# A two-layer graph attention kernel: the first attention's projection by seven half-size products (Strassen, Winograd's form) instead of eight

## The chip, the core and the metric

The kernel runs on one core of a Trainium2 chip. A core has TensorE (PE, matrix products out of SBUF into PSUM), VectorE (DVE), ScalarE (ACT), GpSimd (POOL) and SyncE (SP, here only a queue that issues DMAs). Each engine takes its instructions in the order of the program and waits for semaphores of the others. The metric is the device time of one execution in microseconds; smaller is better. Everything is in fp32.

## The reference, cut to what matters

Sixteen batches, each 1024 nodes with 256 features, go through a layer of two attentions with a residual (`_L0_gnn_ref`) and a layer of one (`_L1_gnn_ref`). The change touches only the first projection in the first layer, `h = inp @ W`, and what hangs on it:

```python
out = relu(x @ mlp1_w + mlp1_b)          # (16, 1024, 512): the kernel's resT, transposed
h = out @ W_fc                           # 1024x512 by 512x512: the projection
f1, f2 = h @ a[:512], h @ a[512:]
e = leaky_relu(f1[:, :, None] + f2[:, None, :], 0.2)    # no mask here
att = softmax(e, axis=2)
h_prime = elu(att @ h)
out = elu(h_prime) + out                 # merged into resT
out = relu(out @ mlp2_w + mlp2_b)        # then the masked attention "a", then layer 1 with "b"
```

## The kernel before

**Tiles.** A batch has NT = 8 tiles of P = 128 nodes. `wfc_sb` is W_fc in four chunks of 128 rows (HC = 4) and two halves g = 0, 1 of 256 columns; each half has one column more (F + 1 = 257), which holds W_fc times a half of `a`, so that f1 comes out as the last column of g = 0 and f2 as that of g = 1. A half of one tile of h is a PSUM group of four matmuls 128x128 by 128x257 (`Dense.project`, L470), and ACT copies it to `h_nat` (L472). For g = 0 POOL takes f1 to `fs` (L474) and puts ones in its place (L475). An fp32 matmul is two rows in the profile.

**The dense attention has no mask**, and is not computed as a matrix: nodes are sorted by f2. `columns` (L478) takes f2 and its maximum, `send` (L243 to L246) turns f2 into a row through PE, ACT and a DMA to DRAM, `row` (L489) brings it back in all partitions, `highest` (L501) finds the maximum over partitions, and `rank` (L514 to L523, once a tile, on DVE) counts how many are smaller. `scatter` (L530, on POOL) writes the rows of h in sorted order to DRAM, `read_sorted` reads them, `sum_before` and `sum_behind` make weighted sums from both ends on DVE, `write_table` and `carry` put these into tables in DRAM, and `gather` (L642, on POOL) fetches for each node the row at its place; `share` (L654) and `mean` (L664 on ACT, L667 on DVE) make the quotient, and `merge` / `merge_end` (L714 to L725) transpose it, apply elu twice and add it to `resT`. `sign` (L553, on ACT) finds each node's place, and needs its f1 from `fs` and the row of f2. `mlp2` (L732) follows. Then come `m.project` of the masked attention "a" (L322, copies on ACT L324), its weights (L375) and products (L385), and the second layer "b" in the same manner. `Norm` makes the layer norm: `stats` (L262), `root` (POOL), `center` (`hn`, L272, DVE) and `turn` (transposes, L282, called nt).

**Order.** All batches are pipelined. Each step is put into one list with a number, `at(lo, hi, steps)`, the list is sorted by that number, and this is the order of the instructions on PE, DVE, ACT, SP and also on POOL. The numbers only order; they are not times. A batch has PERIOD = 142 of them, `base_of(b)` is where the masked part of batch b begins, and a dense part is spread over two periods: for batch b + 2, `dense_rows` puts the projections g = 1 at 86 to 99.5 after `base_of(b)`, and `dense_begin`, with t0 = `base_of(b + 1)`, puts `columns` at t0 - 38.5, `send` and `row` at t0 - 36.8, two projections g = 0 at t0 - 33, `highest` at t0 - 31.5, ranks from t0 - 28 to t0 - 12 and the other six g = 0 at t0 - 21 to t0 - 8. In the same places stand, for batch b + 1, `share` and `mean` at 78 and 92, `merges` at 85 and 98.2, `mlp2` at 102.5 to 116.5 and `m.project` at 135 to 142, and, for batch b + 3, the norm: stats at t0 - 33.5 and t0 - 13, `turn` of the first half at t0 - 22 and of the second at t0 + 0.2, with its `center` 4 before. Batches 0 and 1 are done in a prologue with an order of its own (START).

**Buffers.** PSUM: `mm` four buffers of one bank, used in turn by all products; `tr` two; `bc` one of two banks, used by `send`, `carry` and broadcasts. SBUF: `att` eight tiles of 128x256 for weights of the attentions; `work` has two `part` tiles and two `carry` tiles.

## Time and profile before

| what | value |
|---|---|
| median of 3 runs | 2345.46 us (2337.66 to 2345.5) |
| span of the profiled execution | 2331.2 us, granted clock 0.997 |
| instructions | 30884 |
| projection, matmuls (L470), 2048 rows | 465.7 us busy |
| projection, copies on ACT (L472), 256 | 93.1 us busy, mean 366 ns |
| projection, f1 on POOL (L474 and L475), 128 each | 24.5 and 12.6 us |
| masked products (L385), "b" and "a" | 462.8 and 454.6 us |
| POOL's adds 128x256 (L413), 118 | 98.7 us, mean 836 ns |
| DVE's adds 128x256 (L431), 128 | 54.6 us, mean 427 ns |
| reads and writes of HBM | 226.88 and 126.29 MB |

The span is from the first to the last instruction; the median is 14.3 us above it and the lowest run 6.5 us. A row of a group of instructions names line, engine, operation, out<-in, shapes and count, then busy time and the mean of one in ns, then the time for which the engine stood idle just before them and what ended it. Matmuls overlap, so the busy time of a group of them divided by its count is the time from one to the next, and is smaller than the mean of one. In a timeline the columns are start and length in us, engine, line, operation and count, and in brackets the idle time before and its releaser.

### The profile page before, as it was taken

The page shows a single profiled execution, that of the slowest core. Times are in us where ns is not written, and L with a number is a line of the kernel's source. Part 1 is how long each engine was busy: PE and PEld are TensorE (multiplying, and loading weights), DVE is VectorE, ACT ScalarE, POOL GpSimd, SP SyncE. Part 2 cuts the span into 40 slices and gives each one's busy share as a digit, 9 for nine tenths or more (in the row PEclk, how much of TensorE's full clock was granted, in tenths as well). Part 3 has the DMA queues.
Part 4 walks back from the last instruction along what each step waited for, and adds up shares of the span by engine and source line. Part 5 has one row for each costly group of instructions (what it writes and reads, how often), then busy time and mean ns, then how long its engine had stood idle before and what let it go on. Part 6 is the DMA issues. An engine that isn't in the chain of part 4 may idle for free. (4 is left out here: it accounts for less than half of the span.)

```text
span 2331.2 us, 30884 instructions
## 1 busy us (share of the span) xinstructions
PE 2260.4 (97%) x9962; PEld 1742.7 (75%) x9962; DVE 1625.0 (70%) x4535; ACT 1240.5 (53%) x2745; POOL 950.8 (41%) x1212
## 2 busy tenths in 40 slices
PE   8999999999999999999999999999999999999898
PEld 5666787777868778787776868778786777878666
DVE  6676785766858667675766858567785866858655
ACT  5355645547365563745546365563745547364442
POOL 1153435264443536335263433636335263533420
PEclk9999999999999999999999999999999999999999
DMA  4658356572656736366572756647366582646500
GB/s 172 171 164 208 75 175 168 167 187 88 200 139 178 184 135 183 105 187 153 176 197 89 195 123 181 181 146 182 97 192 160 164 201 101 195 101 191 138 21 27
DMA packets 150714, 355.28 MB, mean 152 GB/s; under 512 B 11200, under 2 KB 62728, under 8 KB 146448
## 3 DMA queue, kind: packets, MB, share of 16 engines
q1 hardware_dynamic: 103936, 189.06, 28.2%
q0 software_dynamic: 45952, 163.99, 26.6%
q8 instruction: 82, 1.34, 0.2%
q14 instruction: 88, 0.72, 0.1%
q10 hardware_dynamic: 656, 0.17, 0.0%
HBM read 226.88 MB, written 126.29 MB: 151 GB/s over the span
## 5 line engine op out<-in xcount | busy, mean ns | idle before, releaser
L385 PE MATMUL ob<-hmb,attb 128*128 128x257 f32 x2048 | 462.8, 383 | 10.8 <-DVE attb L375 6.7
L470 PE MATMUL h<-wfc_sb,resT 128*128 128x257 f32 x2048 | 465.7, 380 | 0.0
L385 PE MATMUL oa<-hma,atta 128*128 128x258 f32 x2048 | 454.6, 381 | 3.4 <-DVE atta L375 3.3
L385 PEld LDWEIGHTS ob<-hmb,attb 128*128 128x128 f32 x2048 | 383.1, 190 | 77.3 <-ACT rb L427 9.6
L385 PEld LDWEIGHTS oa<-hma,atta 128*128 128x128 f32 x2048 | 387.8, 190 | 62.9 <-DVE atta L375 4.5
L470 PEld LDWEIGHTS h<-wfc_sb,resT 128*128 128x128 f32 x2048 | 379.4, 190 | 53.5 <-issue 0.7
L725 POOL TENSOR_TENSOR resT<-resT,e 128x512 f32<-128x512 f32 x128 | 163.7, 1279 | 367.0 <-DVE e L724 325.7
L375 DVE SCALAR_TENSOR_TENSOR atta<-rowsa,qwda,edge 128x256 f32<-128x256 f32 (+1 forms) x520 | 269.0, 547 | 25.0 <-PE oa L385 12.3
L413 POOL TENSOR_TENSOR posa<-posa,onat 128x256 f32<-128x256 f32 x118 | 98.7, 836 | 459.5 <-ACT posa L401 459.4
L375 DVE SCALAR_TENSOR_TENSOR attb<-rowsb,qwdb,edge 128x256 f32<-128x256 f32 (+1 forms) x536 | 248.2, 505 | 8.9 <-PE ob L385 5.5
L456 PE MATMUL m<-hT,w_sb 128*128 128x512 f32 x512 | 236.0, 600 | 0.6 <-ACT posa L401 0.6
L427 ACT ACTIVATE rb<-ob,recb 128x256 f32<-128x256 f32 x128 | 59.0, 475 | 332.7 <-DVE recb L425 323.1
L732 PE MATMUL m<-resT,w_sb 128*128 128x512 f32 x512 | 228.3, 593 | 2.2 <-POOL resT L725 2.2
L642 POOL DMA_INDIRECT got<-coarse,k x124 | 201.3, 1623 | 38.6 <-issue 37.9
L400 ACT ACTIVATE ea<-oa,reca 128x256 f32<-128x256 f32 x128 | 60.7, 474 | 270.7 <-DVE reca L397 262.0
L716 DVE TENSOR_SCALAR e<-hpT 128x512 f32<-128x512 f32 x128 | 88.3, 690 | 129.9 <-PE hpT L714 97.0
L732 PEld LDWEIGHTS m<-resT,w_sb 128*128 128x128 f32 x512 | 93.8, 191 | 103.7 <-issue 91.3
L642 POOL DMA_INDIRECT got<-fine,k x124 | 125.3, 1010 | 104.5 <-DVE attd L688 43.8
L456 PEld LDWEIGHTS m<-hT,w_sb 128*128 128x128 f32 x512 | 92.7, 193 | 96.6 <-issue 92.7
L530 POOL DMA_INDIRECT sorted<-hnat,place x128 | 131.9, 1031 | 39.6 <-issue 21.1
L553 ACT ACTIVATE junk<-r,fs 128x1024 int8<-128x1024 f32 x124 | 142.5, 1149 | 6.8 <-POOL fs L474 5.3
L717 ACT ACTIVATE e<-e 128x512 f32<-128x512 f32 x128 | 80.7, 630 | 82.1 <-DVE e L716 82.0
(189 smaller groups left out, 3443.2 us busy)
## 6 DMA issues: line engine op xcount, KB each, us to landing
xs<-sorted SPq DMA_DIRECT2D x32, 1028.0 KB
fine<-tt SPq DMA_DIRECT2D x32, 1026.0 KB
fine<-xs SPq DMA_DIRECT2D x32, 1026.0 KB
x<-in_x_dram SPq DMA_DIRECT2D x16, 1024.0 KB
xn<-in_x_dram SPq DMA_DIRECT2D x15, 1024.0 KB
out_dram<-x SPq DMA_DIRECT2D x28, 512.0 KB
coarse<-carry SPq DMA_DIRECT2D x32, 256.5 KB
r<-row_r SPq DMA_DIRECT2D x14, 512.0 KB
```

What stands on the lines that cost most here:

```text
L375: nc.vector.scalar_tensor_tensor(a_t[:, :n * P], self.rows[:, i], self.qwd[:, 1, j:j + 1], edge[:, j, i], op0=OP.max, op1=OP.mult)
L385: nc.tensor.matmul(self.out[t][:, :F + self.ONES], lhsT=self.att[t0, j][:, (t - t0) * P:(t - t0 + 1) * P], rhs=self.hm[:, j, 2:2 + F + sel ...
L413: adder.tensor_add(pos, pos, o_nat[:, t, :])
L456: nc.tensor.matmul(ps, lhsT=w1_sb[:, kc, c * P:(c + 1) * P], rhs=hT[:, kc, h * HALF:(h + 1) * HALF], start=(kc == 0), stop=(kc == FC - 1))
L470: nc.tensor.matmul(ps[:, :F + 1], lhsT=self.resT[:, kc, t * P:(t + 1) * P], rhs=wfc_sb[:, kc, g, :], start=(kc == 0), stop=(kc == HC - 1))
L530: made = nc.gpsimd.indirect_dma_start(out=sorted_d[self.b % 2], out_offset=bass.IndirectOffsetOnAxis(ap=self.place[:, t:t + 1], axis=0), i ...
L553: nc.scalar.activation(junk, self.r2, AF.Sign, bias=self.fs[:, 0, t:t + 1], accum_out=self.signs[:, t:t + 1])
L642: nc.gpsimd.indirect_dma_start(out=got[u // n][:, u % n, :], out_offset=None, in_=(coarse_d if coarse else fine_d)[self.b % 2][:, :], in_o ...
L716: nc.vector.tensor_scalar_min(e, ps, 0.0)
L717: nc.scalar.activation(e, e, AF.Exp)
L725: nc.gpsimd.tensor_add(dst, dst, e)
L732: nc.tensor.matmul(ps, lhsT=w2_sb[:, kc, c * P:(c + 1) * P], rhs=self.resT[:, kc, h * HALF:(h + 1) * HALF], start=(kc == 0), stop=(kc == H ...
```

## The change

With A = resT transposed, cut in halves of nodes (1, 2) and of channels, and B = W_fc with its two extra columns, cut in the same way, the four quarters of h = A B are made from seven products instead of eight:

- sums of A, for each of four row blocks u (`sums_of`): S1 = A21 + A22 and S2 = S1 - A11 on DVE, S3 = A11 - A21 and S4 = A12 - S2 on POOL, 128x256 each, into `att` tiles, which become 257 wide;
- sums of B, once (`seven_weights`, four subtractions on POOL); six of the seven factors stay in SBUF, the seventh, B21, goes to DRAM and is loaded again for each batch (`load_b21`, two DMAs of 131.6 KB on SP);
- products (`step`): each is two matmuls 128x128 by 128x257. Steps 1, 6, 5, 3 of a block add into one PSUM buffer, and ACT copies what stands there after each of them to a quarter of `h_nat`. Step 7 of two blocks goes into a `bc` buffer, and `add_pair` adds it on DVE to two quarters (two instructions 128x514 a pair). Steps 2 and 4 have a buffer of their own and are added on DVE to g = 0; f1 and the ones follow on POOL.

Steps 1, 7, 6, 5, 3 (20 a batch) stand at 85.3 to 108 where g = 1 stood; steps 2 and 4 (8 a batch) stand where g = 0 stood, at t0 - 31 and t0 - 22 to t0 - 10. `columns`, `send`, `highest` and the ranks move 4 to 5.7 places back, scatters 2.5, `read_sorted` 2.5, the sums 1.5 to 2, the second `mlp2` 0.7, the `send` of "b" from lo + 24 to 97.3 after `base_of(b)`. The `carry` tiles, the lines and `zero` take `part` tiles.

```diff
+    wfc_more = const.tile([P, 2, 2, F + 1], F32, name="wfc_more")
+    wfc_d = dram.tile([P, 2 * (F + 1)], F32, name="wfc_d")
+
+    def seven_weights():
+        top, low = slice(0, 2), slice(2, HC)
+        b11, b12, b21, b22 = [wfc_sb[:, k, g, :] for k in (top, low) for g in range(2)]
+        nc.sync.dma_start(wfc_d.rearrange("p (k f) -> p k f", k=2), b21)
+        nc.gpsimd.tensor_sub(wfc_more[:, 1], b22, b12)
+        nc.gpsimd.tensor_sub(b12, b12, b11)
+        nc.gpsimd.tensor_sub(wfc_more[:, 0], b22, b12)
+        nc.gpsimd.tensor_sub(b21, b21, wfc_more[:, 0])
...
+    def att_tile(name):
+        return big.tile([P, F + 1], F32, tag="att", name=name, bufs=ATT)
...
-        line = work.tile([NT, P], F32, tag="carry", name=name, bufs=2)
+        line = work.tile([NT, P], F32, tag="part", name=name)
...
-            a_t = big.tile([P, PAIR], F32, tag="att", name=f"att{self.name}_{t0}_{j}", bufs=ATT)
+            a_t = att_tile(f"att{self.name}_{t0}_{j}")
...
-        def project(self, t, g):
+        def sums_of(self, u, which):
+
+            if self.s is None:
+                self.s, self.chain, self.b21 = {}, {}, None
+            one, two = slice(u * P, (u + 1) * P), slice(HALF + u * P, HALF + (u + 1) * P)
+            a11, a12 = self.resT[:, 0:2, one], self.resT[:, 2:HC, one]
+            a21, a22 = self.resT[:, 0:2, two], self.resT[:, 2:HC, two]
+            t = self.s[which, u] = att_tile(f"s{which}_{self.b}_{u}")[:, :PAIR].rearrange(
+                "p (k n) -> p k n", k=2)
+            if which == 1:
+                nc.vector.tensor_add(t, a21, a22)
+            elif which == 2:
+                nc.vector.tensor_sub(t, self.s[1, u], a11)
+            elif which == 3:
+                nc.gpsimd.tensor_sub(t, a11, a21)
+            else:
+                nc.gpsimd.tensor_sub(t, a12, self.s[2, u])
+
+        def load_b21(self):
+            self.b21 = [att_tile(f"b21_{self.b}_{k}") for k in range(2)]
+            for k in range(2):
+                nc.sync.dma_start(self.b21[k], wfc_d[:, k * (F + 1):(k + 1) * (F + 1)])
+
+        def multiply(self, ps, lhs, rhs, start):
+            for k in range(2):
+                nc.tensor.matmul(ps, lhsT=lhs[:, k, :], rhs=rhs[k], start=start and k == 0,
+                                 stop=k == 1, skip_group_check=True)
+
+        def step(self, i, u):
 
             if self.h_nat is None:
                 self.h_nat = big.tile([P, NT, 2, F + 1], F32, tag="seq", name=f"hnat_{self.b}",
                                       bufs=2)
                 self.fs = small.tile([P, 2, NT], F32, tag="fs", name=f"fs_{self.b}")
-            ps = mm_psum(f"h_{self.b}_{t}_{g}")
-            for kc in range(HC):
-                nc.tensor.matmul(ps[:, :F + 1], lhsT=self.resT[:, kc, t * P:(t + 1) * P],
-                                 rhs=wfc_sb[:, kc, g, :], start=(kc == 0), stop=(kc == HC - 1))
-            nc.scalar.copy(self.h_nat[:, t, g, :], ps[:, :F + 1])
-            if g == 0:
-                nc.gpsimd.tensor_copy(self.fs[:, 0, t:t + 1], self.h_nat[:, t, 0, F:])
-                nc.gpsimd.memset(self.h_nat[:, t, 0, F:], 1.0)
+            top, low = (0, 1), (2, 3)
+            b = {1: [wfc_sb[:, k, 0, :] for k in top], 2: self.b21,
+                 3: [wfc_sb[:, k, 1, :] for k in low], 4: [wfc_sb[:, k, 0, :] for k in low],
+                 5: [wfc_sb[:, k, 1, :] for k in top], 6: [wfc_more[:, 0, k, :] for k in top],
+                 7: [wfc_more[:, 1, k, :] for k in top]}[i]
+            one, two = slice(u * P, (u + 1) * P), slice(HALF + u * P, HALF + (u + 1) * P)
+            a = {1: lambda: self.resT[:, 0:2, one], 2: lambda: self.resT[:, 2:HC, one],
+                 3: lambda: self.s[4, u], 4: lambda: self.resT[:, 2:HC, two],
+                 5: lambda: self.s[1, u], 6: lambda: self.s[2, u], 7: lambda: self.s[3, u]}[i]()
+            h = self.h_nat
+            if i in (1, 6, 5, 3):
+                if i == 1:
+                    self.chain[u] = mm_psum(f"h_{self.b}_{u}")
+                ps = self.chain[u][:, :F + 1]
+                self.multiply(ps, a, b, i == 1)
+                t, g = {1: (u, 0), 6: (u + TH, 0), 5: (u + TH, 1), 3: (u, 1)}[i]
+                nc.scalar.copy(h[:, t, g, :], ps)
+            elif i == 7:
+                if u % 2 == 0:
+                    self.pair = bc_psum(f"h7_{self.b}_{u}")
+                self.multiply(self.pair[:, u % 2 * HALF:u % 2 * HALF + F + 1], a, b, True)
+            else:
+                ps = mm_psum(f"h{i}_{self.b}_{u}")[:, :F + 1]
+                self.multiply(ps, a, b, True)
+                t = u if i == 2 else u + TH
+                nc.vector.tensor_add(h[:, t, 0, :], h[:, t, 0, :], ps)
+                nc.gpsimd.tensor_copy(self.fs[:, 0, t:t + 1], h[:, t, 0, F:])
+                nc.gpsimd.memset(h[:, t, 0, F:], 1.0)
+
+        def add_pair(self, u):
+            ps = self.pair.rearrange("p (u f) -> p u f", u=2)[:, :, :F + 1]
+            for g in (1, 0):
+                dst = self.h_nat[:, TH + u:TH + u + 2, g, :]
+                nc.vector.tensor_add(dst, dst, ps)
...
-            carry = work.tile([P, K], F32, tag="carry", name=f"carry_{self.b}_{s}", bufs=2)
+            carry = work.tile([P, K], F32, tag="part", name=f"carry_{self.b}_{s}")
...
     def dense_rows(t0, b):
 
-        for t in range(NT):
-            at(t0 + BETWEEN[t], t0 + BETWEEN[t], [partial(dense[b].project, t, 1)])
+        d = dense[b]
+        for lo, u, i in ((84, 0, 3), (84.5, 1, 3), (86.2, 0, 1), (86.3, 0, 2), (87.4, 1, 1),
+                         (87.5, 1, 2), (88.5, 0, 4), (89.5, 1, 4), (91, 2, 3), (92, 3, 3),
+                         (95.8, 2, 1), (95.9, 2, 2), (97, 3, 1), (97.1, 3, 2), (99, 2, 4),
+                         (100, 3, 4)):
+            at(t0 + lo, t0 + lo, [partial(d.sums_of, u, i)])
+        for lo, i, u in ((85.3, 1, 0), (86.2, 1, 1), (87.1, 7, 0), (88, 7, 1), (89.2, 6, 0),
+                         (90.2, 6, 1), (91.2, 1, 2), (92.2, 1, 3), (93.4, 5, 0), (94.4, 5, 1),
+                         (95.6, 3, 0), (96.6, 3, 1), (98, 7, 2), (99, 7, 3), (100, 6, 2),
+                         (101, 6, 3), (103.6, 5, 2), (104.6, 5, 3), (107, 3, 2), (108, 3, 3)):
+            at(t0 + lo, t0 + lo, [partial(d.step, i, u)])
+        for lo, u in ((96, 0), (106, 2)):
+            at(t0 + lo, t0 + lo, [partial(d.add_pair, u)])
+        at(t0 + 107.5, t0 + 107.5, [d.load_b21])
+
+    def early_steps(d, lo, hi):
+        def group(u):
+            return ([partial(d.sums_of, v, i) for v in (u, u + 1) for i in (3, 1, 2)]
+                    + [partial(d.sums_of, v, 4) for v in (u, u + 1)]
+                    + [partial(d.step, i, v) for i in (1, 7, 6, 5) for v in (u, u + 1)]
+                    + [partial(d.add_pair, u)] + [partial(d.step, 3, v) for v in (u, u + 1)])
+        at(lo, hi, group(0) + group(2))
+
+    def late_steps(d):
+        return [partial(d.step, i, u) for i in (2, 4) for u in range(TH)]
 
     def dense_begin(t0, b):
         d = dense[b]
-        at(t0 - 38.5, t0 - 38.5, [d.columns])
-        at(t0 - 36.8, t0 - 36.8, [d.send, partial(d.row, True)])
-        at(t0 - 31.5, t0 - 31.5, [d.highest])
-        at(t0 - 28, t0 - 12, each(d.rank, range(NT)))
-        at(t0 - 33, t0 - 30.5, [partial(d.project, t, 0) for t in range(2)])
-        at(t0 - 21, t0 - 8, [partial(d.project, t, 0) for t in range(2, NT)])
-        scatters(d, t0 - 18.5, t0 - 4.5)
-        at(t0 - 6, t0 - 6, [d.query])
-        at(t0 - 4, t0 - 4, [d.read_sorted])
+        at(t0 - 32.8, t0 - 32.8, [d.columns])
+        at(t0 - 31.5, t0 - 31.5, [d.send, partial(d.row, True)])
+        at(t0 - 27, t0 - 27, [d.highest])
+        at(t0 - 24, t0 - 8, each(d.rank, range(NT)))
+        late = late_steps(d)
+        at(t0 - 31, t0 - 28, late[:2])
+        at(t0 - 22, t0 - 10, late[2:])
+        scatters(d, t0 - 16, t0 - 2)
+        at(t0 - 4, t0 - 4, [d.query])
+        at(t0 - 1.5, t0 - 1.5, [d.read_sorted])
...
-        at(t0 - 3, t0 - 3, [d.sums_begin])
-        for t, lo in enumerate((27, 25, 18.5, 16.3, 14.1, 12, 9.8, 8.2)):
+        at(t0 - 1, t0 - 1, [d.sums_begin])
+        for t, lo in enumerate((24.5, 22.7, 18, 16, 14, 12, 9.8, 8)):
             at(t0 - lo, t0 - lo, [partial(d.sign, t)])
         for h in range(2):
-            at(t0 + 6.5 + 4 * h, t0 + 6.5 + 4 * h, [partial(d.sums_weights, h)])
-            at(t0 + 7.5 + 5 * h, t0 + 12.5 + 5 * h, each(d.sum_before, tiles(h)))
-        at(t0 + 13, t0 + 13, [partial(d.write_table, 0, 0)])
-        at(t0 + 18, t0 + 18, [partial(d.write_table, 0, 1)])
-        at(t0 + 18, t0 + 32, each(d.sum_behind, range(NT - 1, -1, -1)))
-        at(t0 + 25, t0 + 25, [partial(d.write_table, 1, 1)])
-        at(t0 + 32, t0 + 32, [partial(d.write_table, 1, 0)])
-        at(t0 + 33, t0 + 33, [d.count])
+            at(t0 + 8 + 4 * h, t0 + 8 + 4 * h, [partial(d.sums_weights, h)])
...
-        for i, lo in enumerate((102.5, 104.8, 113, 116.5)):
+        for i, lo in enumerate((102.5, 105.5, 113, 116.5)):
...
-            at(lo + 24, lo + 24, [m.send])
+            at(base_of(b + 1) - 44.7, base_of(b + 1) - 44.7, [m.send])
...
-    at(START + 14.1, START + 14.1, [wfc_columns])
+    at(START + 14.1, START + 14.1, [wfc_columns, seven_weights])
...
-    at(START + 33, START + 50, each(d.project, range(NT), [1]))
+    early_steps(d, START + 33, START + 50)
+    at(START + 49, START + 49, [d.load_b21])
...
-    at(START + 50.5, START + 64, each(d.project, range(NT), [0]))
+    at(START + 50.5, START + 64, late_steps(d))
...
-    at(START + 80, START + 94, each(dense[1].project, range(NT), [1]))
-    at(START + 76, START + 82, each(d.weight, [0], range(NT)))
+    early_steps(dense[1], START + 80, START + 94)
+    at(START + 93.5, START + 96.5, each(d.weight, [0], range(NT)))
...
-        lo = START + 95 + 7.1 * t
+        lo = START + 96.5 + 6.9 * t
...
-    at(START + 123.4, START + 141, each(e.project, range(NT), [0]))
+    at(START + 118.5, START + 118.5, [e.load_b21])
+    at(START + 123.4, START + 141, late_steps(e))
```

## The prediction

> **What bounds the kernel now.** I read the page's busy times first, then the busy time of each engine in stretches of 146 us.
>
> ```profile
> PE 2260.4 (97%) x9962; PEld 1742.7 (75%) x9962; DVE 1625.0 (70%) x4535; ACT 1240.5 (53%) x2745; POOL 950.8 (41%) x1212
> 1026.00:1172.00 146.00, 144.68 (x640) 112.61 (x639) 105.28 (x291) 80.02 (x180) 63.56 (x81) 1.00 0.59 161
> ```
>
> In the second line the columns are busy PE, weight load, DVE, ACT, POOL. In a middle stretch PE is idle for 1.3 us of 146. One batch follows the next after 139.0 us (the row transposition of L243 at 963.32 and again at 1102.35). Next, the groups of instructions:
>
> ```profile
> L470 PE MATMUL h<-wfc_sb,resT 128*128 128x257 f32 x2048 | 465.7, 380 | 0.0
> L322 PE MATMUL pa<-wh_sb,oT 128*128 128x258 f32 x512 | 117.2, 383 | 1.2 <-ACT hma L324 0.9
> ```
>
> A product of L470 is two rows, and a row takes 465.7/2048 = 227 ns of PE. L322 is the nearest row for groups of two chunks, as the new steps are: 117.2/512 = 229 ns. So the rows themselves do get fewer at the same price. Where the saved time goes is read from the timeline, in the stretch from the transposition that sends f2 (call it S, L243) to the transposes of the next input's second half (call it N, L282):
>
> ```profile
> 963.32 0.27 PE L243 MATMUL line_ps<-ident,fs 128*8 128x128 f32 x1
> 965.62 0.24 ACT L245 COPY line<-line_ps 8x128 f32<-8x128 f32 x1
> 967.15 0.34 SPq L489 DMA_DIRECT2D r<-row_r  x1
> 971.15 1.28 DVE L518 TENSOR_SCALAR_CACHE_REDUCE junk<-r,fs 128x1024 uint8<-128x1024 f32 x1
> 987.21 0.22 DVE L523 SCALAR_TENSOR_TENSOR place<-rank 128x1 int32<-128x1 f32 x1
> 988.39 0.63 ACT L324 COPY hma<-pa 128x258 f32<-128x258 f32 x2
> 991.05 1.48 DVE L272 TENSOR_SCALAR hn<-xn,mv,rstd 128x256 f32<-128x256 f32 x4 [1.37 <-POOL rstd L268]
> 992.38 1.04 PE L282 MATMUL nt<-ident,hn 128*128 128x128 f32 x8
> ```
>
> From S to N PE has 29.06 us of work without a gap. Beside it runs a chain on the others: f2 goes out and comes back as a row, eight ranks run on DVE from 971.15 to 987.34, then the statistics, then hn, the last of which ends at 992.53. Both arrive at N together. That this chain has no reserve is seen one stretch later, where the row came later (S to first rank 9.36 us instead of 7.83):
>
> ```profile
> 1250.88 1.28 DVE L518 TENSOR_SCALAR_CACHE_REDUCE junk<-r,fs 128x1024 uint8<-128x1024 f32 x1 [1.53 <-DMA r<-row_r]
> 1269.92 2.01 PE L322 MATMUL pa<-wh_sb,oT 128*128 128x258 f32 x8 [0.41 <-ACT hma L324]
> ```
>
> PE waited at once. So PE is the bound, but in this stretch the rank chain is a second one, level with it.
>
> **Term 1, the products.** Per batch 64 products become 56. Before S there were 32 (g = 1): 64 x 0.2274 = 14.55 us; now steps 1, 7, 6, 5 and 3 run there, 40 products, 80 x 0.229 = 18.32: +3.77. After S there were 32 (g = 0), 14.55; now steps 2 and 4, 16 products, 32 x 0.229 = 7.33: -7.22. Net -3.46 us a batch. The saving is thus taken entirely from the stretch whose second bound is DVE, and more than it.
>
> [...]
>
> **Term 2, the wait at N.** PE now needs 29.06 - 7.22 = 21.84 us from S to N. The chain on DVE, from S:
> - To the first rank. ACT is free for the line's copy (before it stood 2 us behind exponentials), so 0.3 + 0.24 + 0.3 to the DMA's issue, 1.27 to the row's issue (965.88 to 967.15), 3.9 to landing (1246.98 to 1250.88): 6.0. The maximum (L501) stands ahead of the ranks and behind 0.27 + 1.83 (two steps) + 3.55 (mlp2) + 0.27 on PE, then about 0.7 on DVE: 6.6. I take 6.6.
> - Eight ranks: 971.15 to 987.34 less one hn (0.32): 15.85.
> - New on DVE between the ranks: six adds of step 2 and 4, 128x257 out of PSUM. Not in the trace; the nearest row is L431 (128x256, median 0.425, 0.33 from start to start): 6 x 0.38 = 2.3, bounds 2.0 and 2.6.
> - Statistics of four tiles 987.34 to 989.48: 2.14; query 0.2; the first hn 0.4.
>
> Together 27.5 us: if DVE alone decides, PE waits 27.5 - 21.8 = 5.7 us. There is a second way to count: from the first rank to N it took 21.2 us above and 20.9 where PE had waited for ACT; 6.6 + 20.9 + 2.3 = 29.8, a wait of 8.0. The reason is the queue on ACT: the copies of pa stand behind the last sign, the last sign waits for fs of the last tile, fs is copied by POOL after step 4's add, and that add stands on DVE behind seven ranks; with four mm buffers PE can't pass. Step 2's and 4's buffers are themselves released by these adds. I take 29.0, nearer to this, so 7.2 us; bounds 5.7 and 8.0. No gain is possible here: latency and ranks alone, 6.0 + 15.85, equal PE's 21.8.
>
> **Term 3, the wait at S.** Before, columns ran at 960.93, 2.4 us ahead of S. Now the last step 3 is the last work of PE before S and columns needs its copy: 0.22 + 0.36 on ACT, 0.16 on DVE, the hand-overs: 0.85 us, bounds 0.6 and 1.2. Queued behind it are steps 2 and mlp2.
>
> **Term 4, waits inside the first steps.** Steps 1, 6, 5, 3 of a row block add into one PSUM buffer, and between them ACT copies it. ACT is in order and at this place stands behind the shares of the gathers:
>
> ```profile
> 946.39 0.21 DVE L654 TENSOR_TENSOR den<-got,qd 128x4 f32<-128x4 f32 x1 [1.16 <-DMA got<-coarse,k]
> 947.85 0.63 ACT L717 ACTIVATE e<-e 128x512 f32<-128x512 f32 x1 [1.54 <-DVE e L716]
> 949.14 1.32 ACT L664 ACTIVATE part<-got,den 128x513 f32<-128x513 f32 x2
> 950.37 0.35 ACT L472 COPY hnat<-h 128x257 f32<-128x257 f32 x1
> 951.97 0.35 ACT L472 COPY hnat<-h 128x257 f32<-128x257 f32 x1
> ```
>
> The product copied at 951.97 was finished at about 949.5: 2.4 us late, at no cost, since four buffers covered it. Now step 3 of block 0 follows step 5 of block 0 with one step (0.92 us) between: wait 2.4 - 0.9 = 1.5, up to 2.7 if the copy must come after all four parts (till 952.06). Then the pair of step 7 holds the only bc buffer until DVE has done hp, merge_end, two sums and the pair's add (4 x 0.42 + 2 x 0.72 more than before); the send of row b and the third step 7 stand behind: 0 to 2.0, I take 0.5. Together 2.0, bounds 0 and 4.7.
>
> **What costs nothing.** DVE gains 8 sums, 4 pair adds and 8 adds, 8 x 0.425 + 4 x 0.72 + 8 x 0.4 = 9.5 us a batch; before S it was busy for 14.2 of 25 us (938 to 963), now some 20.5 of 29, so only order counts there. Without that cover it would cost up to 6 us. POOL gains 8 x 0.84 = 6.7 (L413), 7.6 of 25 becoming 14.3 of 29. ACT keeps 16 copies. [...] The b21 loads (263 KB) go out on SP once the fourth step 7 is done; SP sat 42 us waiting for the row (591 us over 14), and DMA moves 1 to 3 GB/s there. If they were late, step 2 would be by up to the 3.9 us of the 512 KB row. Reading the sorted rows and the sums move by 1.5 to 2.5 places, but the last scatter comes earlier against N, and DVE idled 4.45 us there for its rows; if it were late, that is the reserve. carry and line now share part's two buffers with the running total; a line is long gone when a carry needs its place, and carry (1032.65) leads the first coarse gather (1056.35) by 23 us. In the prologue PE idles 20.5 of the first 168 us, so two batches' 7 us may not pay, and POOL has four subtractions more (4 x 1.28): 0, bounds -7 and +10.
>
> **Sum.** A steady period: -3.46 + 7.2 + 0.85 + 2.0 = +6.6 us. 14 batches run so (2 to 15): +92. On the span of 2331.2: 2423; the median of the runs is 14.3 above that span (the lowest 6.5), so 2437. Bounds: -3.46 + 5.7 + 0.6 = +2.8 a period, 40 in all, 7 less in the prologue: 2378; -3.46 + 8.0 + 1.2 + 4.7 = +10.4, 146 and 10 more: 2501.
>
> **Rivals.**
> - *PE is the bound throughout, faster.* It pays 14 x 3.46 + 7 = 55 us: 2290. For it: 97%, and 1.3 us idle a period. Against it: S to N has to stay under 21.84 + 3.46 = 25.3 us; my count is 27.5 at least, and a row 1.5 us late was enough for a wait. It decides if the chain is 2.2 us shorter than counted and terms 3 and 4 are near nothing. With part of the gain: 0.14.
> - *A wash.* The chain takes about 25.5 and terms 3 and 4 little: 2345. 0.05.
> - *The PSUM chain is the main cost.* Not one but most of the twelve hand-overs a batch (6, 5, 3 in four blocks) wait for ACT, by 0.4 us more each: 5 us a period, 70 on top: 2507. Against it: the other copies lag by 0.3 to 1.5 us, with 2.7 us of other steps between. 0.07.
> - *The products get no cheaper* (two-chunk groups cost 260 ns a row): 112 x 0.26 against 64 x 2 x 0.2274 gives nothing saved, 48 us more: 2485. L322 speaks against it. 0.04.
> - *The forecast*, 2437: 0.70.
>
> Faster by over 0.5% (about what a measurement of this kernel can tell from no change): 0.14; within: 0.05; slower: 0.81. Between 2350 and 2505 lie 8 in 10.
>
> **What would show it.** Right: PE idle before L282 or L322, on DVE's hn or ACT's hma, 5 to 8 us a period; ranks starting some 6.6 us after S; PE idle before step 3 on ACT's copy. Wrong: S to N below 25 us, or no PE gap before L282 and a period under 139 us.

## The result, and the profile after

The changed kernel takes 2562.99 us (median of 4 runs, 2562.22 to 2567.52) against 2345.48 us before: ratio 1.0927, 95% interval [1.0898, 1.0955]. It is slower, by 217 us where 92 were forecast, and above the range (2378 to 2501 us). The profiled execution has a span of 2561.2 us (before 2331.2, so 230 longer) and a mean granted clock of 0.952 (before 0.997). The difference of the spans is 12.5 us larger than that of the medians, since the profiled execution before was quicker than its median by that much; spread over a period of 139 us this is some 0.7 us, so the losses of a period below are that much too high.

The page's busy times after:

```profile
PE 2319.2 (91%) x9706; PEld 1741.0 (68%) x9706; DVE 1799.3 (70%) x4855; ACT 1252.0 (49%) x2745; POOL 1058.8 (41%) x1344
```

PE has 256 instructions fewer and is busy for 59 us more, while its share fell from 97% to 91%. So two things are to be found: waits, and rows that became slower.

S (now L258, `line_ps`) comes at 305.8, 459.2, ... 2302.4 us: a period of 153.59 us against 139.24 before (the mean of 13 periods). The 230 us of span are then 39.3 up to the first S (266.5 became 305.8), 13 x 14.35 = 186.5 in the periods, and 4.3 behind the last S. From S to N (now L297) it takes 29.3 us (median; before 29.1), so next to nothing was lost there, and nothing gained; from N to the next S 124.3 in place of 110.1.

Inside N to S the loss has one place: from the first transposition of the merges (hpT) to S, where the new steps are. Busy time of this stretch and of S to N; the columns are length, busy PE, weight load, DVE, ACT, POOL, each with its count, then the granted clock. Before:

```profile
937.30:963.30 26.00, 25.66 (x116) 18.54 (x115) 14.80 (x33) 18.59 (x37) 7.64 (x6) 1.00 0.42 101
...
963.30:992.40 29.10, 29.10 (x125) 22.06 (x124) 24.55 (x85) 21.87 (x48) 13.68 (x29) 1.00 0.23 82
```

After:

```profile
1033.30:1073.30 40.00, 33.37 (x131) 23.62 (x130) 26.48 (x55) 22.56 (x46) 16.30 (x18) 0.87 0.27 67
...
1073.30:1102.40 29.10, 25.29 (x89) 17.05 (x90) 23.52 (x83) 17.91 (x37) 11.39 (x29) 0.88 0.24 83
```

26.0 us became 40.0: the whole 14 us of the period. Idle time of PE went from 0.3 to 6.6 us. Its busy time went from 25.7 to 33.4, and 16 rows more, at 227 ns each, explain only 3.6 of these 7.7: the clock is 0.87, so rows run slower in a part of the stretch. PE's timeline in this stretch, after:

```profile
1043.19 1.90 PE L502 MATMUL h<-wfc_sb,s 128*128 128x257 f32 x8
1049.78 3.77 PE L502 MATMUL h<-wfc_sb,s 128*128 128x257 f32 x8 [4.70 <-ACT hnat L527]
1053.85 0.37 PE L258 MATMUL lineb_ps<-ident,qwdb 128*8 128x128 f32 x1 [0.30 <-DVE hnat L544]
1054.65 2.05 PE L502 MATMUL h<-wfc_more,s 128*128 128x257 f32 x4 [0.44 <-ACT lineb L260]
...
1057.35 2.75 PE L502 MATMUL h<-wfc_more,s 128*128 128x257 f32 x8
...
1073.29 0.27 PE L258 MATMUL line_ps<-ident,fs 128*8 128x128 f32 x1 [0.67 <-DVE fs L547]
```

Eight rows take 1.90 us at 1043.19 (238 ns each, the first with its fill) and 3.77 at 1049.78, behind the wait of 4.70 us. The granted clock over the same time says why (the columns are those of the stretches above):

```profile
1045.00:1049.00 4.00, 0.09 (x1) 0.00 (x0) 2.40 (x4) 3.81 (x7) 1.26 (x1) 0.98 0.00 0
1049.00:1053.00 4.00, 3.22 (x8) 2.51 (x8) 3.77 (x6) 1.29 (x4) 1.73 (x2) 0.50 0.00 0
1053.00:1058.00 5.00, 4.27 (x13) 2.89 (x12) 1.80 (x5) 0.63 (x2) 1.10 (x2) 0.50 0.05 8
1058.00:1062.00 4.00, 4.00 (x17) 3.09 (x17) 1.65 (x3) 2.36 (x4) 0.00 (x0) 0.87 0.19 61
```

From about 1049 to 1059 PE runs at half speed. That costs some 4 us: 8 rows 1.9, the next 4 rows 1.0, a block of transpositions 0.5, the 8 rows at 1057.35 0.9. So the ledger of this stretch, from these views: 3.6 us of products that now stand before S, 6.3 of waits, some 4 of half clock, nothing gained behind S. It says where PE's time went, not what each entry would give back if it were gone: in the periods that end with S at 1534.1, 1840.6 and 1994.1 the clock came back sooner (0.95, 0.91 and 0.91 over the stretch, which took 37.5 to 38.0 us), and they are no shorter than the others (152.8 to 153.5 us).

The wait itself comes about as the prediction had it (step 3 waits for ACT's copy of step 5, which stands behind the second half's parts), but it is 4.7 us. DVE's shares, ahead of the parts:

```profile
1041.77 0.63 DVE L723 TENSOR_TENSOR den<-got,qd 128x4 f32<-128x4 f32 x1
1042.43 1.20 DVE L724 TENSOR_TENSOR den<-den,got 128x4 f32<-128x4 f32 x1
...
1043.88 0.44 DVE L726 TENSOR_TENSOR den<-den,qd 128x4 f32<-128x4 f32 x1
```

Three instructions on 128x4 elements take 0.44 to 1.20 us where the same took 0.17 to 0.21 before (from 946.39 on). GpSimd over the same time:

```profile
1040.96 1.42 POOL L493 TENSOR_TENSOR s<-resT,s 128x256 f32<-128x256 f32 x2
1042.33 1.28 POOL L793 TENSOR_TENSOR resT<-resT,e 128x512 f32<-128x512 f32 x1
1043.56 1.43 POOL L491 TENSOR_TENSOR s<-resT 128x256 f32<-128x256 f32 x2
```

The first share ends at 1042.40, where a subtraction of GpSimd ends (1042.38), the second at 1043.63, where the merge's addition to resT ends (1043.61; the kernel before has this one too), the last at 1044.32, about where the first of the two next subtractions ends. ACT behind them:

```profile
1046.24 0.71 ACT L733 ACTIVATE part<-got,den 128x513 f32<-128x513 f32 x1
...
1047.11 1.39 ACT L733 ACTIVATE part<-got,den 128x513 f32<-128x513 f32 x2
1048.66 0.72 ACT L733 ACTIVATE part<-got,den 128x513 f32<-128x513 f32 x1 [0.16 <-DVE hp L736]
1049.29 0.63 ACT L527 COPY hnat<-h 128x257 f32<-128x257 f32 x2
```

Step 5 was done at about 1045.1; its copies run at 1049.29, behind all four parts.

### The profile page after: what moved, and what is told of

Its sections match the earlier page's. It is cut to its first block, busy times and chain, and to the rows that moved or that the text cites. A ratio compares the mean times of both kernels' runs of the same rounds, so it can differ in the third digit from the quotient of the medians.

```text
span 2561.2 us, 31111 instructions
## 1 busy us (share of the span) xinstructions
PE 2319.2 (91%) x9706; PEld 1741.0 (68%) x9706; DVE 1799.3 (70%) x4855; ACT 1252.0 (49%) x2745; POOL 1058.8 (41%) x1344
## 5 line engine op out<-in xcount | busy, mean ns | idle before, releaser
L390 DVE SCALAR_TENSOR_TENSOR atta<-rowsa,qwda,edge 128x256 f32<-128x256 f32 (+1 forms) x520 | 261.1, 534 | 29.2 <-DMA rowsa<-row_a 14.2
L337 PE MATMUL pa<-wh_sb,oT 128*128 128x258 f32 x512 | 165.1, 478 | 54.9 <-DVE hnat L536 53.4
L502 PE MATMUL h<-wfc_sb,s 128*128 128x257 f32 x512 | 147.6, 439 | 64.8 <-ACT hnat L527 64.8
L337 PEld LDWEIGHTS pa<-wh_sb,oT 128*128 128x128 f32 x512 | 114.3, 237 | 106.0 <-DVE hnat L536 79.1
L502 PEld LDWEIGHTS h<-wfc_sb,s 128*128 128x128 f32 x512 | 109.8, 220 | 94.5 <-issue 72.9
```

What stands on the lines that cost most here:

```text
L337: nc.tensor.matmul(ps[:, :2 + F], lhsT=hT[:, c, t * P:(t + 1) * P], rhs=self.w_sb[:, c, 0, :], start=(c == 0), stop=(c == FC - 1))
L390: nc.vector.scalar_tensor_tensor(a_t[:, :n * P], self.rows[:, i], self.qwd[:, 1, j:j + 1], edge[:, j, i], op0=OP.max, op1=OP.mult)
L502: nc.tensor.matmul(ps, lhsT=lhs[:, k, :], rhs=rhs[k], start=start and k == 0, stop=k == 1, skip_group_check=True)
```

## The experiments

All runs beside the two kernels. N to S is the period less the median of S to N; the first S shows the prologue. The runs were taken on several chips, each with the kernel before beside it (2335.1 us for the a runs, 2343.4 for b, 2344.2 for c, 2344.8 for d), so the ratios compare better than the times: by them a1 is as slow as the changed kernel.

| kernel | time, us | ratio to before | period | S to N | N to S | first S |
|---|---|---|---|---|---|---|
| before | 2345.5 | 1 | 139.24 | 29.1 | 110.1 | 266.5 |
| changed | 2563.0 | 1.0927 [1.0898, 1.0955] | 153.59 | 29.3 | 124.3 | 305.8 |
| d1, before, less work behind S | 2344.5 | 0.9996 [0.9977, 1.0016] | 140.03 | 29.5 | 110.5 | 267.0 |
| d2, before, long wait | 2453.3 | 1.0446 [1.0416, 1.0476] | 148.29 | 29.1 | 119.2 | 266.7 |
| d3, before, shorter wait | 2418.3 | 1.0297 [1.0267, 1.0327] | 145.55 | 29.0 | 116.5 | 266.2 |
| a1, wait filled | 2554.5 | 1.0936 [1.0862, 1.1009] | 153.39 | 29.4 | 124.0 | 306.1 |
| a3, no adds of steps 2, 4 | 2516.0 | 1.0771 [1.0739, 1.0802] | 150.51 | 27.9 | 122.6 | 300.8 |
| b1, no sums | 2519.4 | 1.0753 [1.0709, 1.0798] | 151.11 | 30.2 | 120.9 | 295.5 |
| b2, no pair adds | 2534.4 | 1.0817 [1.0757, 1.0877] | 152.21 | 29.6 | 122.6 | 294.1 |
| b3, products only | 2485.1 | 1.0607 [1.0559, 1.0655] | 149.27 | 29.0 | 120.3 | 285.3 |
| b4, shares later | 2525.4 | 1.0779 [1.0735, 1.0823] | 150.98 | 29.5 | 121.5 | 305.9 |
| c1, row sent earlier too | 2539.8 | 1.0831 [1.0801, 1.0861] | 152.30 | 30.5 | 121.8 | 306.9 |
| a2, mlp2 behind S | 2520.2 | 1.0789 [1.0746, 1.0832] | 150.35 | 30.4 | 120.0 | 305.1 |
| c2, c1 and mlp2 behind S | 2500.6 | 1.0664 [1.0637, 1.0691] | 149.11 | 30.6 | 118.5 | 306.6 |
| c3, c2 and the old prologue | 2480.4 | 1.0574 [1.0554, 1.0593] | 149.18 | 32.3 | 116.9 | 281.2 |
| a4, the old prologue alone | 2535.2 | 1.0853 [1.0821, 1.0886] | 152.77 | 29.3 | 123.5 | 288.0 |

### What is the work behind S worth? (d1, a3)

d1 is the kernel before with half of the late products gone, about what the change takes from there (7.3 us):

```diff
-            for kc in range(HC):
+            n = 2 if g == 0 and self.b > 1 else HC
+            for kc in range(n):
```

> The kernel before, with half of the products of its late projection (the ones behind S, batches 2 to 15) left out: two of four per tile, 7.3 us of TensorE in each period behind S, output not the reference's. Nothing else is touched. Theory (behind S the chain of ranks, signs and copies ends at 28 to 29 us whatever TensorE does, so the 7.2 us of products that the change took from there are worth nothing): period 138 to 139.2, S to N 28 to 29.4, 2325 to 2345 us. Rival (TensorE set that stretch before, and only the change's adds made VectorE its bound): S to N 22 to 24 us, period 132 to 134, 2250 to 2280 us.

2344.54 us, ratio 0.9996 [0.9977, 1.0016]: nothing. PE's timeline of one S to N in d1:

```profile
966.60 0.27 PE L243 MATMUL line_ps<-ident,fs 128*8 128x128 f32 x1
...
977.13 5.37 PE L471 MATMUL h<-wfc_sb,resT 128*128 128x257 f32 x24
...
990.66 5.44 PE L322 MATMUL pa<-wh_sb,oT 128*128 128x258 f32 x16 [2.30 <-ACT hma L324]
995.94 1.03 PE L282 MATMUL nt<-ident,hn 128*128 128x128 f32 x8
```

N still comes 29.3 us after S. Of the 7.3 us left out some 4 came back as waits (of pa for ACT's signs and copies above all) and some 2 as slower rows: 16 rows of pa take 5.44 us here, where 229 ns a row makes 3.7. Meanwhile the chain on DVE runs to its end:

```profile
994.31 1.48 DVE L272 TENSOR_SCALAR hn<-xn,mv,rstd 128x256 f32<-128x256 f32 x4 [1.37 <-POOL rstd L268]
```

The last hn ends at 995.79, 29.2 us after S, and N follows at 995.94. The chain of ranks is thus a bound of its own, without any of the change's adds.

a3 leaves out the eight adds of steps 2 and 4 in the changed kernel (L536):

```diff
-                nc.vector.tensor_add(h[:, t, 0, :], h[:, t, 0, :], ps)
```

> The eight adds of steps 2 and 4 out of PSUM on DVE are left out, so the first half of h lacks these products; nothing else changes. Theory (PE waits before N because the four mm buffers are freed by adds that stand between the ranks, and the signs behind them): S to N falls from 29.4 to about 25, a period by 4 to 5 us: 2493 to 2507. Rival (only DVE's own time counts): 6 x 0.38 = 2.3 us a period, 2531. Second rival (ranks alone set N, or ACT does): no change.

2515.98 us, between the two. S to N fell by 1.4 us only, since pa then waited for ACT's copies in place of the adds (58.5 us in all, where it had waited 53.4 for the adds). The other 1.7 us that the period lost lie between N and S; they weren't traced further, and some 0.7 of them go with the chip.

### What does a wait of PE cost? (d2, d3, a1)

d2 and d3 put one wait into each of 13 periods of the kernel before; this is d2, in d3 the 3 is a 1:

```diff
+    def pause(b, n):
+        nc.gpsimd.tensor_scalar_add(hold, dense[b].resT[:, 2, HALF:HALF + NT], 1.0)
+        for _ in range(n):
+            nc.gpsimd.tensor_tensor(hold[:, :TH], hold[:, :TH], power[:, :TH], OP.pow)
+        ps = mm_psum(f"pause_{b}")
+        nc.tensor.transpose(ps[:NT, :P], hold, ident)
...
+        if b > 2:
+            at(lo + 4, lo + 4, [partial(pause, b, 3)])
```

> The kernel before, with one wait of TensorE put into each of its 13 steady periods, among the first MLP's products: a transposition of 128x8 that waits for GpSimd's short chain on the product just copied, 4 to 5.5 us in all; all that is computed stays. Theory (a wait of this length costs its length and then half the clock for some 7 to 9 us, as in the changed kernel): the period grows by 8 to 10 us, 2450 to 2480 us, granted clock near 0.95 to 0.97. Rival (the half clock in the changed kernel has another cause): the clock stays above 0.99 and the period grows by the wait alone, 4 to 5.5 us: 2395 to 2420 us.

> As the long wait, with one step of GpSimd in place of three: 2 to 3 us. Theory (short waits leave the clock full): the period grows by the wait alone, 2370 to 2388 us, clock above 0.99. Rival (every wait brings the half clock): the period grows by 5 to 7 us, 2410 to 2440 us.

The waits came out longer than meant, 89.0/13 = 6.85 and 60.5/13 = 4.65 us, since GpSimd's chain had to wait for ACT's copy of the product (until 964.10 in the period below). So d3 isn't the short wait; by chance it is the length of the one in the changed kernel. That d2's time lies in its theory's range is luck for the same reason: the theory had a wait of 4 to 5.5 us cost twice its length. PE's timeline around one wait in d3:

```profile
957.59 3.17 PE L456 MATMUL m<-hT,w_sb 128*128 128x512 f32 x7
...
965.53 0.38 PE L796 MATMUL pause<-ident,hold 128*8 128x128 f32 x1 [4.66 <-POOL hold L794]
965.70 3.62 PE L456 MATMUL m<-hT,w_sb 128*128 128x512 f32 x4
```

And the clock there, in d3:

```profile
961.00:965.00 4.00, 0.00 (x0) 0.00 (x0) 3.54 (x11) 3.40 (x8) 0.82 (x2) 0.91 1.07 227
965.00:969.00 4.00, 3.47 (x5) 1.40 (x6) 0.00 (x0) 0.00 (x0) 0.47 (x1) 0.50 1.05 221
```

Seven rows take 3.17 us ahead of the wait, four take 3.62 behind it. So the half clock does follow from a wait, in a kernel whose clock was full. Slow rows followed all 13 waits of d3 (3.75 to 5.77 us long): the four rows behind the wait take 2.90 to 3.62 us each time, where four take 1.88 at full clock. In slices of 2 us, taken over three of these periods, the first slice below full clock begins 2.1 to 3.1 us after the wait does, the clock then stands at 0.50 (966 to 970, 1112 to 1116, 1258 to 1260), and the first slice at full clock again begins 4.9 to 6.5 us after PE resumed.

Against the profiled execution of the kernel before, the periods grew by 6.31 (d3) and 9.05 us (d2): the wait and 1.7 to 2.2 us more. By the medians taken beside them (2418.32 and 2453.25 against 2344.78, over 13 periods) they grew by 5.7 and 8.3, which leaves 1.0 to 1.5 us beyond the wait. The changed kernel's rows lose more behind a wait of this length, some 4 us in most periods, since the clock stays at 0.50 for some 10 us, with 0.30 and 0.44 us of further waits in them; whether these prolong it was not tested.

a1 fills the wait of step 3 with eight products of 128x255 that nobody reads:

```diff
+        def fill(self, n):
+            for _ in range(n):
+                nc.tensor.matmul(self.pair[:, F + 1:HALF], lhsT=upto, rhs=w1_sb[:, 0, F + 1:HALF], ...)
...
+        at(t0 + 95, t0 + 95, [partial(d.fill, 8)])
```

> Eight products of 128x255 into unused columns of the pair's buffer are put where PE waits 4.7 us before the third step of block 0 (steady batches only); nobody reads them. Theory (the wait costs twice, since the granted clock stands at 0.50 for some 9 us after it): the 3.6 us of added work fit into the wait, the clock stays at 1.0, the steps behind it run in about 6 us instead of 10.2, and a period of 153.6 us falls by 3 to 4.5: 2500 to 2525 us in place of 2563. Rival (only the hand-overs between ACT, DVE and PE count, the clock costs nothing because PE waits anyway): the time stays within 8 us of 2563. Second rival (the added work delays what follows): up to 50 us more.

2554.47 us, by the ratio no gain: the first rival held. PE's timeline in a1, in the period with the longest rest of the wait (1.93 us; in most it is 1.24):

```profile
1045.37 3.60 PE L542 MATMUL h<-w_sb,upto 128*128 128x255 f32 x16
1050.90 1.97 PE L502 MATMUL h<-wfc_sb,s 128*128 128x257 f32 x8 [1.93 <-ACT hnat L527]
1054.97 0.27 PE L258 MATMUL lineb_ps<-ident,qwdb 128*8 128x128 f32 x1 [2.09 <-DVE hnat L549]
...
1057.33 3.30 PE L502 MATMUL h<-wfc_more,s 128*128 128x257 f32 x8
```

Step 3 ran at about full clock (1.97 us for its eight rows, where 1.90 is full), and PE got to the next hand-over, the pair's buffer, only to wait 2.09 us there for DVE (0.30 before), after which rows slowed down all the same (3.30 us for the eight at 1057.33). A faster PE meets the next queue. So 3.6 us of PE's work could be put in at no cost: PE's wait and the half clock behind it are not what holds S back by themselves.

### Which of the added work makes the waits? (b1, b2, b3)

b1 leaves out all sums of the input (steps 3, 5, 6, 7 read slices of resT in their place):

```diff
-            at(t0 + lo, t0 + lo, [partial(d.sums_of, u, i)])
...
-                 3: lambda: self.s[4, u], 4: lambda: self.resT[:, 2:HC, two],
+                 3: lambda: self.resT[:, 2:HC, one], 4: lambda: self.resT[:, 2:HC, two],
```

> All sixteen sums of the input per batch (8 on VectorE, 8 on GpSimd) are left out; the products of steps 3, 5, 6 and 7 read slices of the input in their place, so the output is not the reference's. TensorE's work, the ACT copies and both kinds of adds stay. Theory (step 3 waits because ACT's copies of step 5 stand behind the shares and the parts, and the shares L723 to L726 take 2.5 us in place of 1.0 beside GpSimd's subtractions): the shares fall back to 0.16 to 0.3 us each, the wait before step 3 falls from 4.7 to about 3 us, the period by 1.5 to 4 us: 2500 to 2540 us. Rival (the sums themselves set the stretch before S): the wait falls below 1 us and the period by 8 us or more: under 2455. Rival (the shares are slow for another reason): they stay at 2.5 us, the time within 10 us of the changed kernel's.

2519.43 us, in the theory's range, with 2.5 us off the period and 10.3 off the first S. DVE's shares in b1:

```profile
1023.76 1.04 DVE L724 TENSOR_TENSOR den<-got,qd 128x4 f32<-128x4 f32 x1 [0.33 <-DMA got<-coarse,k]
1024.84 0.17 DVE L725 TENSOR_TENSOR den<-den,got 128x4 f32<-128x4 f32 x1
...
1025.25 0.16 DVE L727 TENSOR_TENSOR den<-den,qd 128x4 f32<-128x4 f32 x1
```

The second and the last, 1.20 and 0.44 us before, are 0.17 and 0.16 again; the first takes 1.04, and ends as the merge's addition on GpSimd does (1024.78). The four together fell from 2.45 to 1.55 us. The wait for the copy of step 5 fell from 4.7 to 3.9 us in most periods (64.8 in 15 became 56.1 in 16). Sums and shares do hinder each other, but that is a sixth of the wait.

b2 leaves out the two instructions of `add_pair`:

```diff
-            for g in (1, 0):
-                dst = self.h_nat[:, TH + u:TH + u + 2, g, :]
-                nc.vector.tensor_add(dst, dst, ps)
```

> The two additions of step 7 (L544, four of 0.64 us a batch) are left out, and with them the wait of the pair's buffer: the output is not the reference's. Theory (ACT's copy of step 5 sets the wait, VectorE's adds only what comes behind it): the wait before step 3 stays 4.7 us, the 0.3 before lineb_ps and the step 7 behind it go, S comes 0.7 to 1.5 us earlier: 2540 to 2555 us. Rival (VectorE's chain sets the stretch before S): 2.6 us of VectorE less in each period and more behind it: 2505 to 2525.

2534.41 us (2530.28 to 2538.53), between the two ranges. The wait before step 3 stayed (64.8 us in all) and the period fell by 1.4 us, both as the theory had it; the rest is the prologue, where the first S came 11.7 us earlier.

b3 leaves out sums, pair adds and adds together (b1, b2 and a3 in one).

> Sums, pair adds and the adds of steps 2 and 4 are all left out (the output is not the reference's): what stays is seven products of half size in place of eight, with their ACT copies and the changed order. If the products are cheaper as forecast (-3.46 us a period of TensorE) and all that the change lost lies in the work that VectorE and GpSimd got, this kernel stands near or below the kernel before but for its prologue: period 136 to 139 us, 2310 to 2360 us. By the theory (ACT's copies behind the parts make a wait of some 3 us before step 3 without any sum, and the clock falls to half behind it): period 140 to 145, 2370 to 2430. Rival (the work taken away was not what cost): above 2460.

2485.11 us: the theory's 2370 to 2430 was too low, and what its rival said holds. With none of DVE's and GpSimd's new work, seven products, their copies and the new order cost 10.0 us a period still. PE's timeline in b3:

```profile
1003.93 2.77 PE L502 MATMUL h<-wfc_sb,resT 128*128 128x257 f32 x12
1010.61 3.42 PE L502 MATMUL h<-wfc_sb,resT 128*128 128x257 f32 x8 [3.91 <-ACT hnat L528]
```

Here are the 3.6 us of rows moved ahead of S, a wait of 3.91 us behind the parts, and slow rows behind that (eight in 3.42 us in place of 1.90; the granted clock is 0.95 over the stretch from 995.2 to 1031.2). S to N is 29.0, about as in d1. The new work on DVE and GpSimd, which the forecast had at no cost, is the other 4.3 us of the 14.35.

### Can another order take the waits away? (b4, c1, a2, c2, c3)

b4 issues the second half's shares and means behind step 5 and its copies:

```diff
-            lo = t0 + late + 78 + 13.4 * h
+            lo = t0 + late + 78 + (16.2 if h and 0 < b < NB - 1 else 13.4 * h)
...
-            lo = t0 + late + (78.2 + 14 * h if not last(b) else 80 + 12.2 * h)
+            lo = t0 + late + (78.2 + (16.1 if b else 14) * h if not last(b) else 80 + 12.2 * h)
...
-        for lo, u in ((96, 0), (106, 2)):
+        for lo, u in ((94.25, 0), (106, 2)):
```

> Computes everything. The second half's shares and means are issued behind the products of step 5 (and so behind ACT's two copies of it), the first pair add ahead of the means. Theory: ACT copies step 5 as soon as it is done, the wait before step 3 falls from 4.7 to under 1.5 us, the half clock behind it goes, the period falls by 3 to 6 us: 2480 to 2520 us. Rival (as the run with filled waits showed: VectorE and ACT have as much to do before S whatever the order): the wait only moves to the merges of the second half, whose means now come later: 2550 to 2575 us.

2525.39 us. What PE waited for (us in total, times, longest), in the changed kernel:

```profile
PE h L502 <- ACT hnat L527: 64.8, 15, 5.4
```

and in b4:

```profile
PE h L502 <- ACT lineb L260: 51.4, 14, 3.7
...
PE h L502 <- ACT hnat L527: 4.6, 15, 0.4
```

The wait of step 3 is gone, and a new one of 3.7 us stands two steps later, where the row of "b" is copied: ACT's parts now stand ahead of that copy. The period fell by 2.6 us, less than the theory's 3 to 6.

c1 also sends that row earlier, at 86.1, and puts the second mlp2 behind the last step 3:

```diff
-            at(base_of(b + 1) - 44.7, base_of(b + 1) - 44.7, [m.send])
+            go = base_of(b + 1) - (55.9 if b else 44.7)
+            at(go, go, [m.send])
```

> Computes everything; only the order differs from the changed kernel. The run with later shares had moved the wait of 4.7 us to the row of the second masked attention (lineb, 3.7 us: its ACT copy then stood behind four parts). Here that row is also sent earlier, before step 7 of the first block, where ACT has just made its vector, and the second matrix product of the second MLP goes behind the last step 3, ahead of the row transposition S. Theory (the waits and the half clock behind them are all that stands between the forecast's +6.6 us a period and the measured +14.35): waits of TensorE before S fall from 7.1 to about 2 us a period, no half clock before S, the stretch from the transposes to S falls from 124.2 to 114.5 to 116.5 us, the period to 144 to 146: 2430 to 2460 us. Rival (VectorE's and ACT's load before S is the bound): the wait moves once more, period above 149, over 2505 us.

2539.8 us, the rival: the wait moved once more. PE now waited 27.0 us in all for the row (1.8 each in all periods but the first), 41.5 for DVE's hp before the merges (9.8 in the changed kernel), 10.9 for step 5's copies. Though hardly a wait was long any more, the period is no shorter than b4's. In five of the 13 periods the clock was full before S, and they took 150.1 to 153.0 us; the others, at 0.95, took 151.7 to 155.9.

a2 takes the first half's two products of mlp2 (7.2 us) from before S and puts them behind it; c2 is that on top of c1, with the statistics of the next half made while the row is under way, the first step 2 ahead of S and B21 loaded earlier; c3 is c2 with batches 0 and 1 by eight products:

```diff
-        for i, lo in enumerate((102.5, 105.5, 113, 116.5)):
+        for i, lo in enumerate((113, 121, 125, 129) if 0 < b < NB - 1 else
+                               (102.5, 105.5, 113, 116.5)):
```

> Two mlp2 groups of batches 1 to 14 (7.1 us of PE a batch) move from before the row transposition S to behind it, between steps 2 and 4; nothing is left out. Theory (from S to N, 29.4 us, the rank chain on DVE is the bound and PE idles 7.5 us): N to S falls by about 7, S to N grows by 1 at most, a period falls by 6 to 7: 2465 to 2480 us. Rival (the stretch before S is bound by ACT and DVE, not by PE's work): the period falls by less than 2 us, over 2535.

> As the run without the waits, and the first half's two matrix products of the second MLP (3.6 us of TensorE each) go behind S, where TensorE waits some 7 us for the chain of ranks and adds; the statistics of the next input's second half are made while the row is under way, and the first step 2 stands ahead of S. Theory (behind S VectorE's chain of 29 us is the bound and TensorE has 7 us free; before S TensorE is the bound): the stretch before S falls by 7 us, the one behind S stays 29 to 30.5: period 137 to 140 us, 2350 to 2385 us, with the prologue of the changed kernel. Rival (VectorE, 110 us busy in 153, becomes the bound before S too): 2400 to 2450 us.

> As the run with the products behind S, and batches 0 and 1 by eight products, so that the prologue is that of the kernel before. Theory: 18 to 28 us less than that run, 2325 to 2365 us, about the kernel before. Rival (the prologue's loss only moves into the first periods): within 10 us of that run.

2520.23, 2500.61 and 2480.35 us, all above what their theories had, and c2 above its rival too (c3 is 20 us under c2, within the 18 to 28 expected of that step): moving 7.2 us of PE from the long stretch to the one with room shortened the period by 3.2 us, both times (153.59 to 150.35, where some 0.7 goes with the chip, and 152.30 to 149.11, where c2's other changes share in it). S to N grew by 1.1 us in a2. c3 is the best order found and still 5.7% slower than before. From the first merge to S in one period of c3:

```profile
1296.40:1329.90 33.50, 24.39 (x118) 18.43 (x116) 26.22 (x54) 20.58 (x44) 16.28 (x16) 1.00 0.32 80
```

Its waits (us in total, times, longest):

```profile
PE hpT L797 <- DVE hp L751: 40.1, 63, 1.3
PE line_ps L258 <- DVE fs L562: 27.9, 13, 2.2
PE h L517 <- ACT lineb L260: 27.0, 14, 3.7
```

The clock is full here, as in three of the 13 periods (0.95 in the others); PE needs 24.4 us, less than before the change, as 7.2 us of mlp2 stand behind S now; and the stretch takes 33.5. DVE, with 26.2 us (14.8 before the change), is now the busiest engine there, in an order in which PE, ACT and DVE hand over to one another several times per row block. Whether a better order comes under 30 us was not found out.

### The prologue (a4)

a4 does batches 0 and 1 by eight products, as before, and prepares the weights' sums behind them (`seven_weights` at START + 150).

> Batches 0 and 1 in the prologue are projected by eight products in the order of before, and the sums of W are made after them; batches 2 to 15 by seven. Theory (the prologue lost 37 us, S of batch 2 coming at 305.8 instead of 266.5): 30 to 39 us less, 2524 to 2533, and the period stays at 153.6. Rival (the prologue's loss is absorbed or comes from elsewhere): within 8 us of 2563.

2535.22 us, 28 less, but by the ratios (1.0853 against 1.0927) only some 17, where 30 to 39 were expected: the first S comes 17.8 us earlier, and the 0.8 us off the period, where nothing was expected, are about what the chip makes. The first product of the masked attention "a" starts at 190.24 us before, 216.94 in the changed kernel and 197.54 in a4: the prologue itself lost 26.7 us and a4 brings back 19.4. The other 12.6 of the 39.3 up to the first S are the loss of an ordinary period. PE in the first 60 us, before:

```profile
0.00:60.00 60.00, 49.75 (x238) 36.22 (x239) 40.24 (x145) 30.01 (x52) 9.69 (x29) 1.00 0.48 172
```

and after:

```profile
0.00:60.00 60.00, 39.13 (x155) 25.63 (x156) 39.98 (x133) 26.40 (x44) 17.94 (x28) 0.91 0.48 171
```

PE is busy for 10.6 us less, at a lower clock. 10.3 us of its waits are for the masks that DVE makes among the sums and the pair adds (before, PE did not wait for the masks). Without the sums (b1) they are 3.9, and the first S comes at 295.5 instead of 305.8; without the pair adds (b2) they are 3.9 too, and it comes at 294.1. So the work on DVE as a whole delays the masks, not the sums alone.

## Why the prediction was wrong in size

- **Direction and main reason: right.** The products' saving was taken from behind S, where a second chain has no reserve, and so bought nothing. d1 shows it by itself: 0.9996 for as much work taken from the same place.
- **Term 1: right.** 80 rows in place of 64 before S: 3.6 us by the rows (16 at 227 ns), +3.77 forecast; at full clock eight rows still take 1.90 us.
- **Term 2: the number right, in part by luck.** S to N 29.3 us, forecast 29.0; first rank 6.05 us after S (at 1079.34; forecast 6.6); pa waits for the adds. PE's timeline behind the S at 1073.29, after:

```profile
1090.65 1.14 PE L337 MATMUL pa<-wh_sb,oT 128*128 128x258 f32 x4 [1.17 <-DVE hnat L536]
1092.97 1.91 PE L337 MATMUL pa<-wh_sb,oT 128*128 128x258 f32 x4 [1.18 <-DVE hnat L536]
1096.34 6.46 PE L337 MATMUL pa<-wh_sb,oT 128*128 128x258 f32 x20 [1.46 <-DVE hnat L536]
1102.64 1.03 PE L297 MATMUL nt<-ident,hn 128*128 128x128 f32 x8
```

  and DVE's last hn there:

```profile
1099.37 1.58 DVE L287 TENSOR_SCALAR hn<-xn,mv,rstd 128x256 f32<-128x256 f32 x4
```

  That pa waits until the adds of steps 2 and 4 free the buffers is as forecast, but these waits come to 3.8 us, where 7.2 were forecast (5 to 8 by the sign named for it). The last hn ends at 1100.95, 27.7 us after S, about the 27.5 of the first way to count; N comes 1.7 us later, since the last 20 rows of pa take 6.46 us, where 229 ns a row makes 4.6. So the half clock (0.50 from 1094 to 1100), which the forecast did not have, made up for the waits that it had too long.
- **Term 3: right.** 0.67 us, forecast 0.85.
- **Term 4: this step failed.** The place and the cause were right (step 3 behind ACT's copy of step 5, behind the parts), the size was not: step 3 alone waited 4.70 us (4.0 to 5.4 in the 14 batches) where 1.5 were taken and 2.7 allowed, and the whole term was 2.0. Two reasons show in the rows. The lag of the copies was read from a trace in which nothing depended on them, at a single place: b3, with none of the added work, still waits 3.91. And the shares ahead of the parts were taken at their old 0.2 us, where three of them took 0.44 to 1.20 beside GpSimd's instructions: this is the other 0.8 (without the sums, in b1, the wait is 3.9). Taking this wait away doesn't give its length back, though: b4 did so and the period fell by 2.6 us, with a wait of 3.67 two steps later.
- **The clock was not in the sum at all.** Some 4 us of rows at half speed stand behind the wait in most periods. In d3 and d2 waits of 4.65 and 6.85 us (means of 13) cost 1.0 to 2.2 us a period beyond their length, where nothing else was changed; that all 4 count in the period is not shown, and a1 and the periods with less of it speak against it.
- **"What costs nothing" failed for VectorE.** Its load in the stretch was seen ("some 20.5 of 29"), and "up to 6 us" named if the cover were gone. It went from 14.8 in 26.0 us to 26.5 in 40.0. b3 puts the worth of all added work at 4.3 us a period. That a filled wait (a1) and two new orders (b4, c1) mostly moved the waits says that no single one of them is the bound; what is, between N and S, stays open.
- **The prologue failed**: 0 taken, +10 at the most, 26.7 measured. PE's idle time there was read as room, when most of it was PE waiting for DVE (13.5 of the 20.5 us for hn, before), which the sums and the pair adds load further.
- **The 14.3 us from span to median were the profiled execution's own.** After the change the median is 1.8 us above the span. On the spans the forecast missed by 138 us (2423 against 2561.2), on the medians by 126, so this term hid 12 us of the miss.
- **The rivals.** "PE is the bound throughout" is refuted by d1; "the products get no cheaper" by the rows; "the PSUM chain is the main cost" was nearest to the time, but as twelve small hand-overs, when it is one long wait and what follows from it.

In the forecast's terms a period should have read 3.77 - 7.22 + 7.2 + 0.85 + some 10 (6 of waits less those at S, and 4 of half clock) = +14.6, beside the measured 14.35. The 10 is read from the profile after, so this is an account and not a check.

## What to carry to other kernels

Ask of each stretch of a pipelined period whether its work is on the path before counting it as saved: take the work out, as d1 does, before writing the arithmetic that would remove it. An accumulation that is copied between its steps turns copies that were off the path, and whose lateness cost nothing, into links of it (here step 5's copies, for which step 3 waited 4.70 us); their lag has to be read where the copying engine's queue is longest. And when a wait is removed and the time doesn't move, the next hand-over is the bound: look at all engines' busy time in that stretch, not only at the wait.
